# A two-layer graph transformer on one core: the token sums of the seven-product blocks on GpSimd instead of VectorE

## The chip, the cores and the metric

The kernel runs on one core of a Trainium2 chip. The metric is the device time of one execution in microseconds, the median of several runs. TensorE (PE) multiplies, PEld is its weight load, VectorE (DVE) and ScalarE (ACT) work on tiles, GpSimd (POOL) works on tiles too and issues the indirect DMAs (gathers and scatters), SyncE (SP) issues the others.

## The reference

Two layers of a graph transformer over 2708 tokens of width 512, 8 heads, a hidden width of 2048; `adj` is a sparse 0/1 matrix. All numbers are f32.

```python
q, k, v = h @ Wq.T + bq, h @ Wk.T + bk, h @ Wv.T + bv      # 8 heads of 64
scores = where(mask == 0, -1e9, q.k / sqrt(64))
ctx = softmax(scores) @ v
h1 = layer_norm(h + ctx @ Wo.T + bo)
h2 = layer_norm(h1 + relu(h1 @ W1.T + b1) @ W2.T + b2)
```

## The kernel before

**Tiles and blocks.** The tokens are sorted by their number of neighbours and cut into 22 tiles of up to 128. Two tiles make a block, so there are 11 blocks, numbered k = 0 to 10. Layer 0 is done block by block, then layer 1. For each block TensorE does the feed-forward part, and around it the program writes, in the order in which the engines are to do it, the output projection of the next block, the keys and values of the block before for the next layer, and steps of the attention of later blocks.

**Attention.** It runs over lists of neighbours. GpSimd gathers rows of keys and values into the buffers `kv` (line 1113), five buffers of up to two neighbours a token; a gather is issued three steps before it is used. A step of VectorE is: `kv` times `q` (line 1150), its sums per head (`sc`, line 1156, a reduction with one input), and for the step before, values times weights (line 1182) and the accumulation (line 1189). ScalarE makes the weights `p` (line 1169) and scales some of the values (line 1176). When a tile is done its sums follow (lines 1197 to 1212).

**Norms.** Each norm ends on VectorE with line 1273 (the variance, `va`), line 1276 (subtract the mean, times the gain) and line 1281 (times `rd`, plus the shift). In between, GpSimd makes `rd`, the inverse root, from `va` (line 1275). Each block has two norms after the output projection (lines 1455 and 1458 stand ahead of them) and two at its end.

**The seven-product blocks.** In layer 0 the blocks k = 2 to 9 do the second product of the feed-forward part, `relu(..) @ W2.T`, for the first 14 of 16 slices of the hidden width with seven products of half size where eight would be used (a form of Strassen's scheme). The 14 slices are 7 pairs, j = 0 to 6. For slice f TensorE makes `pf` (line 1653, eight instructions, as an f32 product takes two passes), ScalarE the relu `ft` (line 1664). From the two `ft` of a pair, f0 and f1, each with 128 columns for either tile of the block, `sums(j)` makes four sums or differences of 128x128, written to `s[:, 0]`, the upper half of f0 in place, `s[:, 1]` and `s[:, 2]` (lines 1625 to 1628; `s` lies in a tile that the trace calls `forms`). `products(j)` (line 1643) then uses them: `s[:, 1]` in the second product, f0's upper half in the third, `s[:, 0]` in the sixth, `s[:, 2]` in the seventh. Three sums of the weights for each pair are formed once (lines 1592 to 1595) and loaded anew for every block.

**The order around the change.** `sums(j)` is written behind the relu of slice 2j + 2, `products(j)` behind slice 2j + 5. In the loop over f the attention steps, the output projection, and the keys and values are written in between. The last pair's products come after those of slices 14 and 15; then ScalarE and VectorE add up the four PSUM tiles (lines 1695 to 1703), and the two norms follow. So in VectorE's queue the first two sets of sums of a block stand behind the second norm of the block before. TensorE meanwhile does the slices 0 to 5 of the new block, then turns the normed tiles of the block before (line 1293, `tp`), and then needs the first pair's sums.

Of the kernel before, what the change touches and what calls it, by code (L numbers as in the profile page):

```python
# [13 lines left out]
ALU = mybir.AluOpType  # L14
# [4 lines left out]
P = 128  # L19
# [464 lines left out]
def by_edges(ctx: ExitStack, tc: tile.TileContext, x, xT, adj, layers, out, redo):  # L484
# [9 lines left out]
    nc = tc.nc  # L494
# [807 lines left out]
    class Layer:  # L1302
# [310 lines left out]
        def feed_forward_by_seven(self, k, block, hs, hT):  # L1613
# [8 lines left out]
            def sums(j):  # L1622
                f0, f1 = fts[2 * j], fts[2 * j + 1]
                s = self.sums[j % 2]
                nc.vector.tensor_tensor(s[:, 0], f1[:, P:], f0[:, P:], ALU.add)
                nc.vector.tensor_tensor(f0[:, P:], f0[:, :P], f0[:, P:], ALU.subtract)
                nc.vector.tensor_tensor(s[:, 1], s[:, 0], f0[:, :P], ALU.subtract)
                nc.vector.tensor_tensor(s[:, 2], f1[:, :P], s[:, 1], ALU.subtract)

            def products(j):  # L1630
                f0, f1, w, s = fts[2 * j], fts[2 * j + 1], self.w2[j], self.sums[j % 2]
# [17 lines left out]
            for f in range(NFC):  # L1649
                j = f // 2  # L1650
                pf = ps_f.tile([P, DM], F32, tag="f", name="pf")
                for c in range(NC):
                    nc.tensor.matmul(  # L1653
                        pf[:, :W],
                        self.w1[j][:, c, f % 2 * P : f % 2 * P + P],
                        hT[:, c, :],
                        start=(c == 0),
                        stop=(c == NC - 1),
                    )
                if f % 6 < 4:  # L1660
                    ft = dn.tile([P, W], F32, tag="ft", name="ft", bufs=4)
                else:
                    ft = self.more_fts[f % 2]
                nc.scalar.activation(ft, pf[:, :W], AF.Relu, bias=self.b1[:, f : f + 1])  # L1664
                fts.append(ft)
                if f % 2 == 0 and j > 0:
                    sums(j - 1)
                yield None
                if f % 2 and j > 1:
                    products(j - 2)  # L1670
# [411 lines left out]
```

## Time and profile before

| | |
|---|---|
| median of 3 runs (lowest, highest) | 1830.28 us (1830.05, 1832.14) |
| span of the profiled execution, first to last instruction | 1827.1 us |
| around the span, against the median of the runs | 3.2 us |
| granted TensorE clock | 0.999 |
| GpSimd, whole span: busy, instructions | 798.9 us, 745 |
| gathers of `kv` (line 1113): count, busy, mean | 420, 524.0 us, 1248 ns |
| `rd` (line 1275): count, mean | 88, 914 ns |
| the eight seven-product blocks | from 393 to 1005 us of the span |

In the groups of instructions a row gives line, engine, operation, output and inputs, their shapes and the count, then busy time in us and the mean of one in ns, then the idle time ahead of them and who ended it. In the timelines a row gives the start in us, the duration in us, then the same names, and in brackets the idle time before with its releaser. In the waits a row gives who waited for whom, the total, the count and the longest, in us. In the table by stretches each engine has its busy time, in the order PE, PEld, DVE, ACT, POOL, then clock and DMA. Spans on POOL are rough.

### The profile page before, as it was taken

To read this page: it belongs to the slowest core of one execution; us is meant where nothing else is said; L and a number is where in the kernel's file an instruction comes from. 1 tells how busy PE (TensorE), PEld (TensorE's weight loads), DVE (VectorE), ACT (ScalarE), POOL (GpSimd) and SP (SyncE) were. 2 spreads that over 40 slices of the span, in tenths; PEclk is the share of its full clock that TensorE was granted. 3 is DMA by queue.
4 is the path that set the end of the run, shared out by engine and by line. 5 is a ranking of instruction groups with operands and counts; after the bars stand their busy time and mean duration, and the time that the engine had idled before them with its cause. 6 is when DMAs were issued, how large, how long until landed. Compare 5 with 4: busy or idle time off the path is not lost.

```text
span 1827.1 us, 22528 instructions
## 1 busy us (share of the span) xinstructions
PE 1807.5 (99%) x6563; PEld 1162.6 (64%) x6563; DVE 1457.5 (80%) x2447; ACT 949.1 (52%) x3271; POOL 798.9 (44%) x745
## 2 busy tenths in 40 slices
PE   9999999999999999999999999999999999999998
PEld 4444456666777867778677644666666666666666
DVE  5887778988989889898895257887898888889853
ACT  5771435645556545564543213665665565567531
POOL 3334755534455544454430042353464555456302
PEclk9999999999999999999999999999999999999999
DMA  9997987757576676765652876745564664555300
GB/s 340 369 335 256 371 283 245 236 169 241 195 255 228 197 236 196 219 233 181 228 191 70 287 257 248 285 160 180 178 228 150 228 224 169 195 197 194 133 14 21
DMA packets 158061, 393.80 MB, mean 216 GB/s; under 512 B 17514, under 2 KB 60894, under 8 KB 157928
## 3 DMA queue, kind: packets, MB, share of 16 engines
q0 software_dynamic: 70608, 252.12, 40.2%
q1 hardware_dynamic: 77162, 118.55, 18.7%
q10 hardware_dynamic: 10158, 21.61, 3.1%
q8 instruction: 53, 0.87, 0.2%
q14 instruction: 80, 0.66, 0.1%
HBM read 338.78 MB, written 53.44 MB: 215 GB/s over the span
## 4 chain that ended last, share of the span: by engine, by line
PE 89%; DVE 5%; issue 2%; ACT 2%; DMA 1%; POOL 1%; POOLq 0%; SPq 0%; DVEq 0%
PE pf L1523 18%; PE a L1496 17%; PE pf L1653 9%; PE k L620 8%; PE v L620 8%; PE q L620 8%; PE o L620 8%; PE c L1643 4%; PE a L1643 3%; PE tp L1293 2%; DVE sc L1156 1%; DVE kv L1150 1%; DMA forms<-form_d 1%; PE a L1677 1%; PE a L1673 1%
## 5 line engine op out<-in xcount | busy, mean ns | idle before, releaser
L1113 POOL DMA_INDIRECT kv<-kv_d,listed x420 | 524.0, 1248 | 291.2 <-DVE acc L1189 133.9
L1523 PE MATMUL pf<-hT,w 128*128 128x256 f32 (+1 forms) x1792 | 393.2, 367 | 0.1
L1523 PEld LDWEIGHTS pf<-hT,w 128*128 128x128 f32 x1792 | 323.5, 190 | 103.1 <-issue 64.4
L1496 PE MATMUL a<-w,ft 128*128 128x512 f32 x800 | 373.1, 592 | 0.0
L1176 ACT ACTIVATE kv<-kv,p 128x64 f32<-128x64 f32 x1232 | 311.0, 335 | 5.0
L1275 POOL TENSOR_TENSOR rd<-va,mhalf 128x1 f32<-128x1 f32 (+1 forms) x88 | 80.5, 914 | 520.6 <-DVE va L1273 520.5
L1150 DVE TENSOR_TENSOR kv<-kv,q 128x1024 f32<-128x1024 f32 (+1 forms) x222 | 256.9, 1157 | 13.3 <-DMA q<-q_d,ident_i 10.9
L1156 DVE TENSOR_REDUCE sc<-kv 128x16 f32<-128x1024 f32 (+1 forms) x222 | 257.9, 1162 | 7.6
L1189 DVE TENSOR_TENSOR acc<-acc,kv 128x1024 f32<-128x1024 f32 (+2 forms) x178 | 205.4, 1154 | 37.6 <-ACT kv L1176 23.0
L1653 PE MATMUL pf<-hT,w 128*128 128x256 f32 x1024 | 233.1, 379 | 1.6 <-ACT ft L1664 1.6
L1496 PEld LDWEIGHTS a<-w,ft 128*128 128x128 f32 x800 | 150.1, 190 | 113.2 <-issue 101.3
L1653 PEld LDWEIGHTS pf<-hT,w 128*128 128x128 f32 x1024 | 193.9, 190 | 35.4 <-issue 7.9
L1534 ACT ACTIVATE ft<-pf,b 128x256 f32<-128x256 f32 (+1 forms) x208 | 95.0, 459 | 197.6 <-PE pf L1523 195.2
L1169 ACT ACTIVATE p<-sc,listed 128x8 f32<-128x8 f32 x420 | 104.0, 296 | 147.2 <-DVE sc L1156 135.7
L620 PE MATMUL o<-wo,cT 128*128 128x512 f32 x336 | 151.0, 593 | 1.0 <-ACT cT L1298 1.0
L1664 ACT ACTIVATE ft<-pf,b 128x256 f32<-128x256 f32 x96 | 44.9, 468 | 160.5 <-PE pf L1653 160.5
L1182 DVE TENSOR_TENSOR kv<-kv,p 128x512 f32<-128x512 f32 (+1 forms) x178 | 123.4, 693 | 4.5 <-ACT p L1169 4.3
L620 PEld LDWEIGHTS o<-wo,cT 128*128 128x128 f32 x336 | 63.4, 190 | 74.7 <-issue 65.5
L745 DVE MAX8 tops<-code 128x8 f32<-128x247 f32 (+2 forms) x242 | 78.6, 400 | 28.3 <-ACT code L740 28.3
L1281 DVE SCALAR_TENSOR_TENSOR h<-h,rd,ln_b 128x512 f32<-128x512 f32 (+1 forms) x88 | 65.9, 749 | 39.5 <-POOL rd L1275 39.5
L1220 ACT ACTIVATE cx<-acc,su 128x64 f32<-128x64 f32 (+1 forms) x352 | 88.2, 333 | 12.9 <-DVE su L1212 7.4
L1455 DVE TENSOR_TENSOR h<-o,xb 128x512 f32<-128x512 f32 (+1 forms) x44 | 30.3, 688 | 80.0 <-PE o L620 65.0
(232 smaller groups left out, 2323.5 us busy)
## 6 DMA issues: line engine op xcount, KB each, us to landing
aj<-in_adj SPq DMA_DIRECT2D x42, 677.0 KB, 6.3
forms<-form_d SPq DMA_DIRECT2D x168, 128.0 KB, 4.2
kv_d<-kvs ACTq DMA_DIRECT2D x21, 512.0 KB, 5.5
xg<-in_xT SPq DMA_DIRECT2D x19, 512.0 KB, 7.4
w<-in_W SPq DMA_DIRECT2D x16, 512.0 KB, 6.2
kv<-kv_d,listed POOLq DMA_INDIRECT x420, 6.3
zT_d<-zT SPq DMA_DIRECT2D x22, 256.0 KB, 5.1
xb_d<-h SPq DMA_DIRECT2D x21, 256.0 KB, 5.7
```

Of the source, the lines that this page charges most:

```text
L620: nc.tensor.matmul(o[:r], xs(c), wm[:, c, :], start=(c == 0), stop=(c == NC - 1))
L1113: return nc.gpsimd.indirect_dma_start(out=to, out_offset=None, in_=table[:, :], in_offset=bass.IndirectOffsetOnAxis(ap=s, axis=0), bounds_ ...
L1150: nc.vector.tensor_tensor(kv[:r, :c, :DM], kv[:r, :c, :DM], self.q[:r].unsqueeze(1).to_broadcast([r, c, DM]), ALU.mult,)
L1156: nc.vector.tensor_reduce(self.sc[:r, s0 : s0 + c, :], kv[:r, :c, :DM].rearrange("p s (h d) -> p s h d", d=DK), AX.X, ALU.add,)
L1169: nc.scalar.activation(p[:r, s, :], self.sc[:r, s, :], AF.Exp, bias=minus[:r, g, s : s + 1])
L1176: nc.scalar.activation(to[:, i, hd], kv[:r, i, DM + h * DK : DM + (h + 1) * DK], AF.Copy, scale=p[:r, s0 + i, h : h + 1],)
L1182: nc.vector.tensor_tensor(to[:, 0, :].rearrange("p (h d) -> p h d", d=DK), kv[:r, 0, DM:].rearrange("p (h d) -> p h d", d=DK), p[:r, s0, : ...
L1189: nc.vector.tensor_tensor(self.acc[:r, :c, :], self.acc[:r, :c, :], kv[:r, :c, DM:], ALU.add)
L1496: nc.tensor.matmul(a[:r, cols], fts[f][:, c0 : c0 + r], self.w2[f // 2][:, f % 2, cols], start=(f == 0), stop=(f == NFC - 1),)
L1523: nc.tensor.matmul(pf[:, :w], self.w1[f // 2][:, c, f % 2 * P : f % 2 * P + P], hT[:, c, :w], start=(c == 0), stop=(c == NC - 1),)
L1643: nc.tensor.matmul(to, left, right, start=start, stop=stop)
L1653: nc.tensor.matmul(pf[:, :W], self.w1[j][:, c, f % 2 * P : f % 2 * P + P], hT[:, c, :], start=(c == 0), stop=(c == NC - 1),)
```

## The change

The four additions and subtractions of `sums(j)` are issued by GpSimd instead of VectorE; operands, shapes and the place in the program stay.

```diff
             def sums(j):
                 f0, f1 = fts[2 * j], fts[2 * j + 1]
                 s = self.sums[j % 2]
-                nc.vector.tensor_tensor(s[:, 0], f1[:, P:], f0[:, P:], ALU.add)
-                nc.vector.tensor_tensor(f0[:, P:], f0[:, :P], f0[:, P:], ALU.subtract)
-                nc.vector.tensor_tensor(s[:, 1], s[:, 0], f0[:, :P], ALU.subtract)
-                nc.vector.tensor_tensor(s[:, 2], f1[:, :P], s[:, 1], ALU.subtract)
+                nc.gpsimd.tensor_tensor(s[:, 0], f1[:, P:], f0[:, P:], ALU.add)
+                nc.gpsimd.tensor_tensor(f0[:, P:], f0[:, :P], f0[:, P:], ALU.subtract)
+                nc.gpsimd.tensor_tensor(s[:, 1], s[:, 0], f0[:, :P], ALU.subtract)
+                nc.gpsimd.tensor_tensor(s[:, 2], f1[:, :P], s[:, 1], ALU.subtract)
```

The instructions of TensorE and ScalarE keep their order. First VectorE at the start of block k = 5, before, from the second closing norm of block 4 on:

```order
L1276 SCALAR_TENSOR_TENSOR h<-h,mv,ln_g 128x512
L1281 SCALAR_TENSOR_TENSOR h<-h,rd,ln_b 128x512
L1625 TENSOR_TENSOR forms<-ft 128x128
L1626 TENSOR_TENSOR ft<-ft 128x128
L1627 TENSOR_TENSOR forms<-forms,ft 128x128
L1628 TENSOR_TENSOR forms<-ft,forms 128x128
L1625 TENSOR_TENSOR forms<-ft 128x128
L1626 TENSOR_TENSOR ft<-ft 128x128
L1627 TENSOR_TENSOR forms<-forms,ft 128x128
L1628 TENSOR_TENSOR forms<-ft,forms 128x128
L1150 TENSOR_TENSOR kv<-kv,q 128x2x512
L1156 TENSOR_REDUCE sc<-kv 128x16
```

VectorE at the same place now:

```order
L1276 SCALAR_TENSOR_TENSOR h<-h,mv,ln_g 128x512
L1281 SCALAR_TENSOR_TENSOR h<-h,rd,ln_b 128x512
L1150 TENSOR_TENSOR kv<-kv,q 128x2x512
L1156 TENSOR_REDUCE sc<-kv 128x16
L1182 TENSOR_TENSOR kv<-kv,p 128x512
L1189 TENSOR_TENSOR acc<-acc,kv 128x1024
```

The two sets of sums (j = 0 and 1) are gone; the attention step follows the norm directly. GpSimd at the same place, before:

```order
L1275 TENSOR_TENSOR rd<-va,mhalf 128x1 x2
L1113 DMA kv<-kv_d_111,listed 128x1024 x2
L1113 DMA xb<-in_x,ident_i 128x512 x2
L1113 DMA kv<-kv_d_111,listed 128x1024 x4
L1113 DMA q<-q_d_113,ident_i 128x512
```

and now:

```order
L1275 TENSOR_TENSOR rd<-va,mhalf 128x1 x2
L1625 TENSOR_TENSOR forms<-ft 128x128
L1626 TENSOR_TENSOR ft<-ft 128x128
L1627 TENSOR_TENSOR forms<-forms,ft 128x128
L1628 TENSOR_TENSOR forms<-ft,forms 128x128
L1625 TENSOR_TENSOR forms<-ft 128x128
L1626 TENSOR_TENSOR ft<-ft 128x128
L1627 TENSOR_TENSOR forms<-forms,ft 128x128
L1628 TENSOR_TENSOR forms<-ft,forms 128x128
L1113 DMA kv<-kv_d_111,listed 128x1024 x2
L1113 DMA xb<-in_x,ident_i 128x512 x2
```

The sums stand behind both `rd` of the closing norms and ahead of the gathers. Later in the same block GpSimd had, behind the scatters of the next layer's keys and values, six gathers and the two `rd` of the norms after the output projection:

```order
L1113 DMA kv<-kv_d_111,listed 128x1024 x2
L1076 DMA kv_d_112<-kvs,ident_i 2708x1024 x2
L1113 DMA kv<-kv_d_111,listed 128x1024 x6
L1275 TENSOR_TENSOR rd<-va,mhalf 128x1 x2
L1113 DMA kv<-kv_d_111,listed 128x1024 x4
```

and has now, from the fourth of these gathers on:

```order
L1113 DMA kv<-kv_d_111,listed 128x1024 x4
L1625 TENSOR_TENSOR forms<-ft 128x128
L1626 TENSOR_TENSOR ft<-ft 128x128
L1627 TENSOR_TENSOR forms<-forms,ft 128x128
L1628 TENSOR_TENSOR forms<-ft,forms 128x128
L1113 DMA kv<-kv_d_111,listed 128x1024 x2
L1275 TENSOR_TENSOR rd<-va,mhalf 128x1
L1625 TENSOR_TENSOR forms<-forms 128x128
L1626 TENSOR_TENSOR forms<-forms 128x128
L1627 TENSOR_TENSOR forms<-forms 128x128
L1628 TENSOR_TENSOR forms<-forms 128x128
L1275 TENSOR_TENSOR rd<-va,mhalf 128x1
```

The sums of j = 4 stand ahead of the last two gathers and the first `rd`, those of j = 5 between the two `rd`.

## The prediction

> **What bounds the kernel now.** I read the page's busy times first, then the stretch in which the edited lines run (393 to 1005 us, the eight seven-product blocks), then what TensorE waits for inside it.
>
> ```profile
> PE 1807.5 (99%) x6563; PEld 1162.6 (64%) x6563; DVE 1457.5 (80%) x2447; ACT 949.1 (52%) x3271; POOL 798.9 (44%) x745
> 393.00:1005.00 612.00, 605.68 (x2492) 453.72 (x2491) 525.72 (x878) 324.84 (x1211) 273.04 (x225) 1.00 0.62 203
> PE o L615 <- ACT cT L1298: 2.4, 1, 2.4
> PE tp L1293 <- DVE h L1281: 1.8, 2, 1.0
> PE pf L1653 <- ACT ft L1664: 1.6, 2, 0.8
> ```
>
> The reader is to see that TensorE is the bound, in the whole span and in this stretch (605.68 of 612 us). The last three rows are its waits of any size there: 5.8 us, of which VectorE causes 1.8 (two waits for a normalized tile, line 1281). No row has TensorE waiting for lines 1625 to 1628. So taking work off VectorE can give back about 2 us, while any operand that comes later than TensorE wants it costs its full lateness.
>
> How late may the sums come? I looked for the tightest of the seven pairs of a block and found the first: its sums are made at the block's start, right behind the two norms that end the block before. Here is block k = 5, as VectorE, GpSimd and the weight loads have it.
>
> ```profile
> 631.39 0.74 DVE L1276 SCALAR_TENSOR_TENSOR h<-h,mv,ln_g 128x512 f32<-128x512 f32 x1
> 632.58 0.75 DVE L1281 SCALAR_TENSOR_TENSOR h<-h,rd,ln_b 128x512 f32<-128x512 f32 x1 [0.45 <-POOL rd L1275]
> 633.25 0.28 DVE L1625 TENSOR_TENSOR forms<-ft 128x128 f32<-128x128 f32 x1
> ...
> 633.78 0.28 DVE L1627 TENSOR_TENSOR forms<-forms,ft 128x128 f32<-128x128 f32 x1
> ...
> 635.36 1.22 DVE L1150 TENSOR_TENSOR kv<-kv,q 128x1024 f32<-128x1024 f32 x1
> 636.61 1.22 DVE L1156 TENSOR_REDUCE sc<-kv 128x16 f32<-128x1024 f32 x1
> 631.62 0.93 POOL L1275 TENSOR_TENSOR rd<-va,mhalf 128x1 f32<-128x1 f32 x1 [1.25 <-DVE va L1273]
> 634.26 0.41 PEld L1643 LDWEIGHTS c<-forms 128*128 128x128 f32 x2
> ```
>
> Call E the end of the last norm's line 1281: 632.58 + 0.75 = 633.33. The third add (line 1627) makes s[:,1], the weights of the second product; it ends at 633.78 + 0.28 = 634.06, E + 0.73, and TensorE loads it at 634.26. The slack is 0.20 us. The first and the last of the eight blocks:
>
> ```profile
> 405.95 0.28 DVE L1627 TENSOR_TENSOR forms<-forms,ft 128x128 f32<-128x128 f32 x1
> 406.29 0.39 PEld L1643 LDWEIGHTS c<-forms 128*128 128x128 f32 x2
> 937.75 0.28 DVE L1627 TENSOR_TENSOR forms<-forms,ft 128x128 f32<-128x128 f32 x1
> 939.09 0.41 PEld L1643 LDWEIGHTS c<-forms 128*128 128x128 f32 x2
> ```
>
> That is 0.06 and 1.06; read off the same two rows, blocks k = 2 to 9 have 0.06, 0.05, 1.37, 0.20, 0.21, 0.69, 0.09 and 1.06 us, 3.73 together. The later pairs of a block are not as tight: see the last one of block 5, below.
>
> **The change, part by part.** Removed from VectorE: 56 times four adds.
>
> ```profile
> L1626 DVE TENSOR_TENSOR ft<-ft 128x128 f32<-128x128 f32 x40 | 11.9, 297 | 1.4
> ```
>
> This is the slowest of the eight groups of these lines; 224 adds at 0.297 us are at most 66 us of VectorE time. What of that is on the path? In block 5 the stretch from the last attended norm to the block's closing sums (line 1696) shows it:
>
> ```profile
> 680.95 0.69 DVE L1455 TENSOR_TENSOR h<-o,xb 128x512 f32<-128x512 f32 x1 [2.35 <-PE o L620]
> 685.34 0.29 DVE L1625 TENSOR_TENSOR forms<-ft 128x128 f32<-128x128 f32 x1
> 686.47 1.22 DVE L1150 TENSOR_TENSOR kv<-kv,q 128x1024 f32<-128x1024 f32 x1
> 690.37 1.22 DVE L1189 TENSOR_TENSOR acc<-acc,kv 128x1024 f32<-128x1024 f32 x1 [0.82 <-ACT kv L1176]
> 695.20 1.25 DVE L1189 TENSOR_TENSOR acc<-acc,kv 128x1024 f32<-128x1024 f32 x1 [0.58 <-ACT kv L1176]
> 687.43 0.47 ACT L1664 ACTIVATE ft<-pf,b 128x256 f32<-128x256 f32 x1 [4.28 <-PE pf L1653]
> 696.51 0.41 PEld L1643 LDWEIGHTS c<-forms 128*128 128x128 f32 x2
> ```
>
> VectorE waits for TensorE at 680.95 and twice for ScalarE, which itself had waited 4.28 us for TensorE. The 1.13 us of one set of sums (685.34 to 686.47) would only lengthen the wait at 690.37. (These are the sums of the last pair, done before 686.6 and loaded at 696.51: 10 us of room.) So I put the gain from the relief at zero, except after block 2, where no such wait lies between the last sums and the block's end: there 1.13 less about 0.5 for collisions (below), 0.6 us.
>
> Added to GpSimd: 224 adds. None of this shape in f32 is in the trace; the nearest are a 128x128 add of integers and a 128x512 one of f32.
>
> ```profile
> L734 POOL TENSOR_TENSOR aj<-aj,diag 128x128 int32<-128x128 int32 x20 | 8.7, 433 | 29.6 <-DMA aj<-in_adj 29.6
> L958 POOL TENSOR_TENSOR kvs<-kvs,bk 128x512 f32<-128x512 f32 x20 | 25.4, 1272 | 52.4 <-ACT kvs L956 43.3 <-issue 4.7 <-DMA aj<-in_adj 4.3
> ```
>
> I take 0.43 us, since the shape is the same; a quarter of the second row would be 0.32. By the skill an add would be longer: the Trainium skill, GPSIMD Engine Reference, section Engine selection, puts two-input elementwise work about 2x slower on GpSimd than on VectorE, which makes an estimate of 0.59 us an add and, by the steps below, 10.6 us in place of 6.7. The trace has 1.5x (0.43 against 0.297), and I go by it.
>
> Moved: the adds now stand in GpSimd's queue directly behind the two rd instructions (line 1275) of the block's start, and VectorE goes from line 1281 straight to line 1150. Do the engines get in each other's way? These rows say so:
>
> ```profile
> 447.83 0.58 POOL L1275 TENSOR_TENSOR rd<-va,mhalf 128x1 f32<-128x1 f32 x1
> 142.42 1.25 POOL L958 TENSOR_TENSOR kvs<-kvs,bk 128x512 f32<-128x512 f32 x1
> 142.60 1.64 DVE L771 TENSOR_TENSOR hot<-count,by 128x528 f32<-128x528 f32 x1
> ```
>
> An rd that runs alone takes 0.58 us. The one at 631.62 started while line 1276 (two inputs in SBUF) ran, took 0.93, and ended at 632.55, 0.42 after line 1276's end at 632.13: of its 0.58, 0.16 had passed before it was held. The other way, line 771 started 0.18 after a GpSimd add and took 1.64 for 528 columns, ending 0.57 after that add. So a GpSimd add and a two-input VectorE instruction do not overlap; the second waits for the first. Who goes when both wait? A scatter of GpSimd, which takes 1.02 alone, between two such instructions:
>
> ```profile
> 436.28 1.02 POOL L1076 DMA_INDIRECT kv_d<-kvs,ident_i  x1 [0.30 <-issue]
> 437.61 1.60 POOL L1076 DMA_INDIRECT kv_d<-kvs,ident_i  x1 [0.31 <-issue]
> 437.11 1.23 DVE L1189 TENSOR_TENSOR acc<-acc,kv 128x1024 f32<-128x1024 f32 x1
> 438.25 1.22 DVE L1150 TENSOR_TENSOR kv<-kv,q 128x1024 f32<-128x1024 f32 x1
> ```
>
> The second scatter ended 0.87 after line 1189 and was not held by line 1150 as well, which was ready by then: the one that has waited longer goes first, and so they take turns. If nothing were held, the three adds would end at 632.55 + 3 x 0.43 = 633.84, before 634.06, and nothing would be late. The Trainium skill, SBUF — State Buffer, section Who interferes with whom, has the holding as a rule: a VectorE instruction with two SBUF inputs and a GpSimd instruction that reads SBUF share an interface, and whichever is issued first keeps it to its end. By that rule the time would come out as forecast below; the trace agrees in both directions (0.93 against 0.58, and 1.64).
>
> The steps at the block's start, from E: add 1 is held by line 1281 until E and needs 0.43 - 0.16 = 0.27 more: E + 0.27. Line 1150, ready since E - 0.08 as the first add was before, runs its remaining 1.14: E + 1.41. Add 2, held behind it, 0.27: E + 1.68. Add 3 runs beside line 1156, which has one input, in 0.43: E + 2.11. Before it was E + 0.73, so s[:,1] comes 1.38 us later. Less each block's slack, TensorE waits 1.32, 1.33, 0.01, 1.18, 1.17, 0.69, 1.29 and 0.32, which is 7.3 us; less 0.6 for the relief in front of block 3, **6.7 us**. The fourth add (s[:,2], the seventh product) has five products of 0.43 more and is hidden by them.
>
> Bounds: if no add is ever held, nothing is late and the 1.8 us of waits for line 1281 could go: -2 us. If add 3 too is held by a full 1.22 us instruction and then needs 0.27, it ends at E + 3.17, 2.44 later than before: 8 x 2.44 - 3.73 - 0.6 = +15 us. I take 6.7, which has a row for each hold.
>
> What else is queued behind the adds on GpSimd:
>
> ```profile
> 671.29 1.40 POOL L1113 DMA_INDIRECT kv<-kv_d,listed  x1 [0.30 <-issue]
> 675.76 0.93 POOL L1275 TENSOR_TENSOR rd<-va,mhalf 128x1 f32<-128x1 f32 x1 [0.42 <-DVE va L1273]
> 683.65 0.92 POOL L1275 TENSOR_TENSOR rd<-va,mhalf 128x1 f32<-128x1 f32 x1 [6.96 <-DVE va L1273]
> 688.95 1.04 PE L1293 MATMUL tp<-ident,h 128*128 128x128 f32 x8
> ```
>
> The fifth set of sums stands between the gather that ends at 672.69 and the rd at 675.76, with two gathers between. Four adds of 0.8 us would move that rd by about 3 us, to 679; its reader on VectorE is followed by line 1455, which waits for TensorE until 680.95 anyway. The sixth set stands between the two rd's and has until 683.65. TensorE reads the normed tiles at 688.95. So this is hidden, with about 3 us to spare. Gathers are issued three steps ahead of their reader; 3 us of delay stays inside that.
>
> **Against the runs.** The profiled span is 1827.1 us, 3.2 under the median of the runs (1830.28), which holds what lies around it. I add to the median: 1830.28 + 6.7 = 1837.0 us. A measurement of this kernel can tell 0.2%, 3.7 us, from no change.
>
> **Rivals.**
> - *Back to back, no change.* GpSimd, once it has the interface, keeps it: adds 2 and 3 follow at 0.43 each, E + 1.13, only 0.40 later than before. Stalls: 0.34 + 0.20 + 0.19 + 0.31, block 3 covered by its relief: 1.0 us, 1831.3. For it: GpSimd's adds have no other engine to wait for. Against: line 1150 is ready before add 2 is. Chance 0.20.
> - *VectorE's relief counts, faster.* If ScalarE's waits shrink with VectorE's, the norms come 1 us earlier in each block, the late sums are covered and most of the waits of 2.4, 1.8 and 1.6 us go: some -5, 1825.3. Against: the rows at 680.95, 687.43 and 690.37. Chance 0.07.
> - *GpSimd's queue becomes the bound, far slower.* If four adds take over 5 us instead of some 3, the rd's are late. At 6 us: sums to 678.69, two gathers of 1.3, rd to 682.3, sums to 688.3, rd to 689.2, line 1281 to 690.0, 0.6 behind the second half of the reads from 688.95; seven blocks, 4 us. At that pace three adds at the block's start take 4.5, ending 3.0 later than before: 8 x 3.0 - 3.73 = 20. Together +24, 1854. Chance 0.06.
> - That the change doesn't do what it says is excluded: the instruction order shows the 224 adds on GpSimd.
>
> **How the numbers follow.** The forecast has 0.67, nearly all of it over 3.7 us (0.05 within). Faster 0.07; same 0.20 + 0.05 = 0.25; slower 0.62 + 0.06 = 0.68. The range takes the likely bound above (+15 us) and the no-change rival, down to 1829.5, leaving out most of the two outer rivals: 1829.5 to 1845.5.
>
> **What would show it.** Right: in the changed profile, a wait of about 1.2 us of TensorE or its weight loads for line 1627 at the start of most blocks, none at the later pairs; line 1150 at 0.27 behind E or its duration near 1.5; the second add lasting over 1 us; rd in the attended norms 2 to 4 us later with nothing behind it. Wrong: line 1627 ending by E + 1.2; or waits for lines 1625 to 1628 at pairs other than the first; or the closing norms of a block sooner after the last product than now.

## The result and the profile after

| | before | changed |
|---|---|---|
| median of 20 runs each (lowest, highest), one chip | 1829.72 us (1828.66, 1835.99) | 1835.51 us (1832.47, 1840.51) |
| ratio, 95% interval | | 1.0029 (1.0021 to 1.0036) |
| median of two later groups of runs | 1829.25; 1830.04 us | 1834.84; 1835.07 us |
| their ratios | | 1.0030 (1.0018 to 1.0042); 1.0026 (1.0017 to 1.0035) |

The change costs 5.3 us (0.0029 x 1829.72), between 3.8 and 6.6. The forecast was +6.7 us. The two later groups are two of the experiments below, with the changed kernel untouched. One execution of the kernel with two more adds ahead of the fourth pair (below) took 11025 us and is left out of its ratio; the median of its other five is 1837.48 us.

The busy times of the page, then the stretch of the eight seven-product blocks, which is 621 us long in the profiled execution and was 612:

```profile
PE 1809.9 (99%) x6563; PEld 1161.7 (63%) x6563; DVE 1418.9 (77%) x2223; ACT 948.3 (52%) x3271; POOL 934.6 (51%) x969
```

```profile
393.00:1014.00 621.00, 609.98 (x2496) 453.69 (x2495) 488.89 (x656) 326.21 (x1219) 410.68 (x449) 1.00 0.61 201
```

VectorE gave up 36.8 us of busy time in the stretch (525.72 to 488.89), GpSimd took on 137.6 (273.04 to 410.68), and TensorE still has 99% of the span. The profiled spans differ by 8.8 us (1827.1 and 1835.9), more than the medians: this execution took 1837.65 us, 2.1 above its kernel's median, and some 2 us of the difference lie ahead of 393 us, where nothing was changed. The later profiles of the same kernel have spans of 1831.9 and 1831.0 us.

TensorE's waits between 393 and 1015 us, and below them the same for its weight loads over the whole span:

```profile
PE c L1643 <- POOL forms L1627: 3.3, 6, 0.6
PE o L615 <- ACT cT L1298: 2.3, 1, 2.3
PE c L1643 <- DMA forms<-form_d: 2.0, 2, 1.3
PE pf L1653 <- ACT ft L1664: 1.7, 2, 0.8
PE tp L1293 <- DVE h L1281: 1.7, 2, 1.1
```

```profile
PEld c L1643 <- POOL forms L1627: 5.9, 7, 1.0
```

The first row is the new one: six waits for line 1627, the third add, now on GpSimd. The rows for lines 615, 1653 and 1293 stand as they were (2.4, 1.6, 1.8 before). Now block 5 again, VectorE, GpSimd, weight loads and TensorE from the last norm on:

```profile
637.67 0.94 DVE L1281 SCALAR_TENSOR_TENSOR h<-h,rd,ln_b 128x512 f32<-128x512 f32 x1 [0.45 <-POOL rd L1275]
638.54 1.48 DVE L1150 TENSOR_TENSOR kv<-kv,q 128x1024 f32<-128x1024 f32 x1
640.05 1.22 DVE L1156 TENSOR_REDUCE sc<-kv 128x16 f32<-128x1024 f32 x1
...
637.61 0.45 POOL L1625 TENSOR_TENSOR forms<-ft 128x128 f32<-128x128 f32 x1
638.14 0.79 POOL L1626 TENSOR_TENSOR ft<-ft 128x128 f32<-128x128 f32 x1
638.89 1.43 POOL L1627 TENSOR_TENSOR forms<-forms,ft 128x128 f32<-128x128 f32 x1
640.40 0.46 POOL L1628 TENSOR_TENSOR forms<-ft,forms 128x128 f32<-128x128 f32 x1
...
640.38 0.30 PEld L1643 LDWEIGHTS c<-forms 128*128 128x128 f32 x2 [0.98 <-POOL forms L1627]
...
639.20 0.60 PE L1643 MATMUL a<-forms,ft 128*128 128x256 f32 x2
640.38 0.70 PE L1643 MATMUL c<-forms 128*128 128x256 f32 x2 [0.58 <-POOL forms L1627]
640.92 0.59 PE L1643 MATMUL c<-forms,ft 128*128 128x256 f32 x2
```

An add that nothing holds takes 0.45 us. Add 1 started 0.06 ahead of line 1281 and wasn't held; line 1281 was, and took 0.94 instead of 0.75. Add 2 then ended at 638.93, 0.32 behind the end of line 1281 at 638.61: held by it. Line 1150 was held by add 2 (1.48 instead of 1.22). Add 3 stood beside line 1150, which ended at 640.02, and ended itself 0.30 after that. The two engines took turns, one instruction each, and all eight blocks have the same four end times within 0.02 us: -0.55, 0.32, 1.71 and 2.24 after the end of line 1281.

The same three products of TensorE before the change:

```profile
634.04 0.60 PE L1643 MATMUL a<-forms,ft 128*128 128x256 f32 x2
634.48 0.59 PE L1643 MATMUL c<-forms 128*128 128x256 f32 x2
634.91 0.59 PE L1643 MATMUL c<-forms,ft 128*128 128x256 f32 x2
```

The distance from the first product to the second was 0.44 us and is now 1.18: the second starts 0.74 late, although its weight load waited 0.98. From the first to the third it was 0.87 and is now 1.72: the third starts 0.85 late. The missing 0.1 us lies inside the second product, whose two passes start 0.32 us apart instead of 0.22.

### The profile page after: what moved, and what is told of

It reads as the page before. It is cut to its first block, busy times and chain, and to the rows that moved or that the text cites. A ratio compares the mean times of both kernels' runs of the same rounds, so it can differ in the third digit from the quotient of the medians.

```text
span 1835.9 us, 22631 instructions
## 1 busy us (share of the span) xinstructions
PE 1809.9 (99%) x6563; PEld 1161.7 (63%) x6563; DVE 1418.9 (77%) x2223; ACT 948.3 (52%) x3271; POOL 934.6 (51%) x969
## 4 chain that ended last, share of the span: by engine, by line
PE 80%; DVE 7%; issue 4%; ACT 4%; POOL 3%; DMA 2%; SPq 0%; POOLq 0%; DVEq 0%; ACTq 0%
PE pf L1523 17%; PE a L1496 17%; PE k L620 8%; PE v L620 8%; PE pf L1653 7%; PE o L620 7%; PE q L620 6%; PE c L1643 4%; PE a L1643 3%; ACT kv L1176 2%; PE tp L1293 2%; DVE kv L1150 1%; DVE sc L1156 1%; DMA forms<-form_d 1%; POOL rd L1275 1%
## 5 line engine op out<-in xcount | busy, mean ns | idle before, releaser
L1113 POOL DMA_INDIRECT kv<-kv_d,listed x420 | 504.3, 1201 | 200.1 <-issue 105.8
L1150 DVE TENSOR_TENSOR kv<-kv,q 128x1024 f32<-128x1024 f32 (+1 forms) x222 | 262.6, 1183 | 15.5 <-DMA q<-q_d,ident_i 12.2
L1455 DVE TENSOR_TENSOR h<-o,xb 128x512 f32<-128x512 f32 (+1 forms) x44 | 30.3, 689 | 81.2 <-PE o L620 67.9
```

The source lines that it names most:

```text
L1113: return nc.gpsimd.indirect_dma_start(out=to, out_offset=None, in_=table[:, :], in_offset=bass.IndirectOffsetOnAxis(ap=s, axis=0), bounds_ ...
L1150: nc.vector.tensor_tensor(kv[:r, :c, :DM], kv[:r, :c, :DM], self.q[:r].unsqueeze(1).to_broadcast([r, c, DM]), ALU.mult,)
```

## The experiments

My theory, A: the price lies only where a block starts, since TensorE asks for the first pair's sums there at once, and it comes from the two engines' turns; the other pairs' sums cost nothing, and VectorE's relief is worth nothing. Rival B: the price is spread over all sets, through GpSimd's longer queue or through VectorE instructions that last longer beside its adds. Rival C: the relief of VectorE is worth something, and the price at the blocks' starts hides it. Each ratio is against the kernel before on the same chip: its median is 1829.22 us beside the first four kernels below (late pairs, first pairs, one-input instructions, two more adds ahead of the first pair), 1830.04 beside the two more adds run again, the ten more and the changed kernel of that group, and 1829.25 beside the rest. In the edited kernels the numbers of the lines behind the edit are one to three higher.

### Late pairs on GpSimd, the first two on VectorE

```diff
-                nc.gpsimd.tensor_tensor(s[:, 0], f1[:, P:], f0[:, P:], ALU.add)
+                by = nc.vector if j < 2 else nc.gpsimd
+                by.tensor_tensor(s[:, 0], f1[:, P:], f0[:, P:], ALU.add)
...
```

> GpSimd makes the sums of pairs 2 to 6 of each block (40 of the 56 sets), VectorE those of pairs 0 and 1 as before the change. Theory A (only the set that stands at a block's start has a price, because TensorE waits for it and for no other; relief of VectorE is worth next to nothing): the time falls back to that of the kernel before, 1829.7 us within 1.5, and PEld shows no wait for line 1627 on GpSimd at a block's start (5.9 us in 7 places in the changed kernel). Theory B (the price lies on all sets alike, through GpSimd's longer queue or through VectorE's instructions that last longer beside it): 40/56 of the +5.3 us stay, about 1833.5. Theory C (relief of VectorE counts and was only covered by the price at the blocks' starts): faster than before, below 1827.

Measured: 1827.86 us, ratio 0.9994 (0.9985 to 1.0003). All of the price is gone, with 40 of the 56 sets still on GpSimd. TensorE's waits in the stretch, and the table's row for 393 to 1005 us:

```profile
PE o L615 <- ACT cT L1298: 2.2, 1, 2.2
PE pf L1654 <- ACT ft L1665: 1.6, 2, 0.8
PE tp L1293 <- DVE h L1281: 1.3, 2, 0.9
```

```profile
393.00:1005.00 612.00, 606.75 (x2502) 454.84 (x2501) 496.22 (x720) 324.88 (x1212) 378.49 (x385) 1.00 0.61 204
```

The three rows are those of before. VectorE is 29.5 us less busy (525.72 to 496.22), GpSimd 105 more, and TensorE does about as much in the 612 us as before (606.75, 605.68). Against B. The median lies 1.4 us under that of before, but the interval holds 1.

### The complement: the first two pairs on GpSimd

```diff
+                by = nc.gpsimd if j < 2 else nc.vector
+                by.tensor_tensor(s[:, 0], f1[:, P:], f0[:, P:], ALU.add)
...
```

> The complement: GpSimd makes the sums of pairs 0 and 1 of each block (16 of 56 sets), VectorE all others. Theory A: nearly the whole price is there, +4 to +5.5 us, 1834 to 1835.3, and PEld waits some 6 us for line 1627 in 7 or 8 places, as in the changed kernel. Theory B: 16/56 of +5.3 us, +1.5, about 1831.2. Theory C: slower than the changed kernel, since the price stays and the relief goes: above 1836.

Measured: 1836.35 us, ratio 1.0037 (1.0023 to 1.0051): 16 of the 56 sets carry the whole price. The weight loads' wait:

```profile
PEld c L1644 <- POOL forms L1628: 5.8, 7, 1.0
```

It is the changed kernel's (5.9, 7 times, line number shifted by one). The median lies above what A named (1835.3), but the interval, +4.2 to +9.3 us, holds it. Theory C asked for a time above 1836 as well, so this run alone doesn't part A from C; the run without sums does.

### One-input instructions where line 1150 stood

```diff
                 s = self.sums[j % 2]
+                if j == 0:
+                    for _ in range(3):
+                        spread(self.e2)
                 nc.gpsimd.tensor_tensor(s[:, 0], f1[:, P:], f0[:, P:], ALU.add)
```

> The changed kernel with three more one-input instructions on VectorE (the kernel's own statistics instruction over a constant that it reads anyway, into a scratch tile, about 0.69 us each) ahead of sums(0) in each block, so that VectorE's two-input line 1150 doesn't stand beside GpSimd's adds at a block's start. Theory A with the hold (add 3 took 1.43 us because a two-input VectorE instruction ran beside it): add 3 lasts 0.45 to 0.6 us, the adds end about 0.8 us after the end of line 1281 and not 2.24, PEld's waits for line 1627 fall from 5.9 us to under 1.5, and the time comes back to within 2 us of the kernel before, 1830 to 1832. Rival (GpSimd's add is slow by itself, or starts late after the semaphore): the wait stays near 1 us in a block and the time at 1835 to 1837.

Measured: 1829.17 us, ratio 1.0002 (0.9993 to 1.0011). All 56 sets are on GpSimd, VectorE even does three instructions more in each block, and the price is gone. Block 5:

```profile
632.96 0.44 POOL L1628 TENSOR_TENSOR forms<-ft 128x128 f32<-128x128 f32 x1
633.48 0.79 POOL L1629 TENSOR_TENSOR ft<-ft 128x128 f32<-128x128 f32 x1
634.23 0.46 POOL L1630 TENSOR_TENSOR forms<-forms,ft 128x128 f32<-128x128 f32 x1
...
633.01 0.94 DVE L1281 SCALAR_TENSOR_TENSOR h<-h,rd,ln_b 128x512 f32<-128x512 f32 x1 [0.45 <-POOL rd L1275]
633.88 1.87 DVE L1286 BATCH_NORM_STATS2 st<-ln_b 128x6 f32<-128x512 f32 x3
635.66 1.20 DVE L1150 TENSOR_TENSOR kv<-kv,q 128x1024 f32<-128x1024 f32 x1
...
634.74 0.41 PEld L1646 LDWEIGHTS c<-forms 128*128 128x128 f32 x2
```

Adds 1 and 2 last as long as in the changed kernel. Add 3 (here line 1630), beside the statistics with one input, lasts 0.46 instead of 1.43 and ends 0.74 after line 1281, where it ended 0.73 after it before the change; the weights are loaded without a wait. So the price was the hold of add 3 by line 1150, all of it as far as the interval tells (-1.3 to +2.0 us). GpSimd's longer adds, add 2's hold and line 1281's 0.19 us cost nothing that can be measured.

### Two more adds ahead of the first pair, and ahead of the fourth

```diff
+                if j == 0:
+                    for _ in range(2):
+                        nc.gpsimd.tensor_tensor(s[:, 2], f1[:, P:], f0[:, P:], ALU.add)
                 nc.gpsimd.tensor_tensor(s[:, 0], f1[:, P:], f0[:, P:], ALU.add)
```

> The changed kernel with two more adds of 128x128 on GpSimd ahead of add 1 of pair 0 of each block, which repeat add 1 into a part of the tile that add 4 overwrites. Theory A (the chain of four adds at a block's start stands on the path, and nothing absorbs a delay of it): two unheld adds of 0.45 us come on top, the second sum is ready some 0.9 us later in each of eight blocks, +6 to +8 us over the changed kernel, about 1842; where one of them is held by line 1150 as well, up to 1849. Theory B (the price is spread over GpSimd's queue, and the block start is no special place): 16 adds more on 224, +0.4 us, about 1836.

Measured: 1842.44 us, ratio 1.0069 (1.0056 to 1.0083), 7 us over the changed kernel. The weight loads' waits, then block 5:

```profile
PEld c L1646 <- POOL forms L1630: 13.3, 8, 2.0
```

```profile
638.02 1.44 POOL L1628 TENSOR_TENSOR forms<-ft 128x128 f32<-128x128 f32 x1
639.53 0.46 POOL L1629 TENSOR_TENSOR ft<-ft 128x128 f32<-128x128 f32 x1
639.95 0.45 POOL L1630 TENSOR_TENSOR forms<-forms,ft 128x128 f32<-128x128 f32 x1
```

The third of six adds meets line 1150 and lasts 1.44; the fourth and fifth run beside line 1156 in 0.46 and 0.45. s[:,1] is ready 2.66 after the end of line 1281, 0.95 later than in the changed kernel; eight times that is 7.6, and the loads' wait rose by 7.4 (5.9 to 13.3).

The same two adds with `j == 3` in place of `j == 0`:

> The changed kernel with two more adds on GpSimd as in the run that put them ahead of pair 0 (that one cost some 7 us over the changed kernel), but ahead of pair 3, whose sums were ready 3.5 us or more before TensorE asked for them. Theory A (a delay counts only where no slack is left): the time of the changed kernel, within 1.5 us, about 1835. Theory B (GpSimd's queue, or what its adds do to VectorE, has the price wherever they stand): the same +7 us as at pair 0, about 1842.

Measured: 1837.53 us, ratio 1.0046 (1.0033 to 1.0059), and beside it the changed kernel untouched:

> The changed kernel once more, beside the others of this group: +4 to +6.5 us over the kernel before, some 1835. It also tells whether the waits of TensorE for the forms that come from DRAM by DMA (PEld 2.8 us in the first profile after, 2.4 with the first pairs alone on GpSimd, 1.3 in the other two experiments on the changed kernel) belong to the change: if they follow from it, PEld's wait for forms lies again above 2 us; if they vary from run to run, anywhere between 0.4 and 3.

Measured: 1834.84 us, ratio 1.0030 (1.0018 to 1.0042). The wait of its weight loads for forms that come by DMA is 0.9 us here; it was 2.8 in the first profile of the same kernel, and the third lists none. So it varies from run to run and isn't the change's. (A further 0.9 us in this profile is put down to line 1625, but the load that waits there, for pair 2 of block 7, reads none of the sums that ran then.)

The 2.7 us between the two kernels were more than A's 1.5 and less than B's 7; no row of the trace named a wait for pair 3. So it was run again on another chip, with the changed kernel beside it and a stronger dose:

> The two more adds ahead of pair 3 once more. Theory A: within 1.5 us of the changed kernel beside it, the 2.7 us of the first time being the runs' scatter; if they were a price, +2 to +3.5 us again.

> The changed kernel as the measure for the run with ten more adds in a block, on the same chip: 1834 to 1836, ratio to the kernel before 1.003.

Measured: 1835.89 us, ratio 1.0025 (1.0014 to 1.0035), against 1835.07 us, 1.0026 (1.0017 to 1.0035). Here the difference is 0.8 us: two adds cost 7 us ahead of the first pair, and by the medians 0.8 and 2.7 us ahead of the fourth, which these runs hardly tell from nothing. The traces hint at a small price. The loads' wait for the first pair's sums is the same in both profiles with the two adds, and 5.9 in all three of the changed kernel:

```profile
PEld c L1646 <- POOL forms L1630: 6.6, 7, 1.0
```

The 0.7 us more all lie at block 9, where the load waits 0.94 instead of 0.20.

### Ten more adds in a block

The edit of the last section with `j > 1`: 80 more adds in all.

> The two more adds on GpSimd ahead of pair 3 came out 2.7 us above the changed kernel beside them (medians), inside the two intervals but more than theory A's 1.5; their trace shows no wait for the sums of pair 3. Here two more adds stand ahead of each of the pairs 2 to 6, 80 in all, five times the dose, each pair's slack being 3.5 us or more. If GpSimd's load has a price away from the block's start, five times 2.7: +13 us over the changed kernel, about 1848. Theory A: the changed kernel's time within 2 us, about 1835 to 1837, with PEld's waits for GpSimd's sums still near 6 us.

Measured: 1845.04 us, ratio 1.0074 (1.006 to 1.0088), 10 us over the changed kernel beside it. Here theory A fails in the strict form that I gave it. The waits in the stretch, of this kernel and of the changed kernel beside it:

```profile
PE tp L1293 <- DVE h L1281: 5.8, 5, 1.7
PE c L1646 <- POOL forms L1630: 3.9, 7, 0.6
PE c L1646 <- DMA forms<-form_d: 2.5, 4, 1.0
```

```profile
PE c L1643 <- POOL forms L1627: 3.3, 6, 0.6
...
PE tp L1293 <- DVE h L1281: 1.7, 2, 1.1
```

The sums' own wait hardly moved (3.9 against 3.3), and no late pair's sums are waited for. What grew is the wait for normed tiles (1.7 to 5.8; four of the five waits stand at a block's start) and that for forms that come by DMA (no such row to 2.5; as the first profile of the changed kernel had 2.0, this one may be scatter). So GpSimd's load does have a price away from the first pair. It isn't one price for every add: the 224 of the change cost nothing that can be told once the hold at the block's start is gone (the one-input run), and these 80 cost 10 us. But those came off VectorE, and these came on top. Where the price sets in isn't shown: at 10 us for 80, the 16 adds of the last section would cost 2.

VectorE's waits between 393 and 1015 us tell in part where the late norms come from; this kernel first, then the changed kernel beside it:

```profile
DVE h L1281 <- POOL rd L1275: 47.0, 25, 8.5
DVE h L1281 <- POOL rd L1275: 30.7, 25, 4.5
```

The 16.3 us more all lie in the seven waits for the first `rd` of a block's attended norms, each 1.7 to 4.0 us longer, while line 1150 lasts 1.26 us on average instead of 1.23. So GpSimd's queue ahead of `rd` looks like the larger part, rather than the holds in VectorE's attention steps; it wasn't tried by itself.

### The sums left out

Pairs 2 to 6 of seven blocks get no sums (35 of 56 sets; their products use old ones), the rest on VectorE.

```diff
+                if j > 1 and k > FORMED + 1:
+                    return
+                nc.vector.tensor_tensor(s[:, 0], f1[:, P:], f0[:, P:], ALU.add)
...
```

> The sums back on VectorE as before the change, and those of pairs 2 to 6 in seven of the eight blocks left out (35 of the 56 sets; the products of these pairs use old sums, so the output isn't the reference's). This takes VectorE's load off, about 35 x 1.19 = 42 us, without putting it anywhere else, and leaves the set at a block's start where it was. Theory A (relief of VectorE is worth next to nothing, since TensorE waits for VectorE in few places): 1827 to 1829.7, 0 to -2 against before. Theory C (relief counts, and GpSimd's own price hid it): -5 us or more, below 1825.

Measured: 1828.36 us, ratio 0.9998 (0.999 to 1.0007).

```profile
393.00:1005.00 612.00, 606.47 (x2504) 455.19 (x2503) 493.94 (x740) 325.44 (x1212) 270.68 (x225) 1.00 0.61 203
```

VectorE lost 31.8 us of work in the stretch (525.72 to 493.94) that no other engine took up, and the time stayed, within 1.8 us. Theory C asked for 5 us or more: it falls.

### Only the first pair on VectorE

```diff
+                by = nc.vector if j < 1 else nc.gpsimd
...
```

> VectorE makes the sums of pair 0 of each block alone, GpSimd those of the other six pairs (48 of 56 sets). Theory A (the one set at a block's start carries the whole price): the time of the kernel before, within 1.5 us, no PEld wait for GpSimd's sums, though six sevenths of the change stay. If pair 1 had a share in the price as well, which the run with pairs 0 and 1 on VectorE couldn't tell: above 1831, with PEld waits for its sums. Theory B (spread over all sets): 48/56 of the price, 1834.

Measured: 1831.14 us, ratio 1.0013 (1.0004 to 1.0021): +2.4 us, between 0.7 and 3.8. A had asked for no price, and B for 1834. Block 5:

```profile
633.12 0.45 POOL L1626 TENSOR_TENSOR forms<-ft 128x128 f32<-128x128 f32 x1
633.65 0.79 POOL L1627 TENSOR_TENSOR ft<-ft 128x128 f32<-128x128 f32 x1
634.40 0.50 POOL L1628 TENSOR_TENSOR forms<-forms,ft 128x128 f32<-128x128 f32 x1
...
633.18 0.94 DVE L1281 SCALAR_TENSOR_TENSOR h<-h,rd,ln_b 128x512 f32<-128x512 f32 x1 [0.45 <-POOL rd L1275]
634.05 0.54 DVE L1626 TENSOR_TENSOR forms<-ft 128x128 f32<-128x128 f32 x1
634.62 0.43 DVE L1627 TENSOR_TENSOR ft<-ft 128x128 f32<-128x128 f32 x1
634.97 0.28 DVE L1628 TENSOR_TENSOR forms<-forms,ft 128x128 f32<-128x128 f32 x1
...
635.30 0.30 PEld L1644 LDWEIGHTS c<-forms 128*128 128x128 f32 x2 [0.44 <-DVE forms L1628]
```

The adds on GpSimd here are those of pair 1. TensorE doesn't wait for them, but they run at the same moment as VectorE's adds of pair 0 and hold those: 0.54 and 0.43 instead of 0.28 each, so that s[:,1] ends 1.13 after line 1281 and not 0.73, and the weight load waits 0.44. The loads' wait for these sums is 2.6 us in 6 places. So the place that costs is not a set of sums but a moment: two-input work on GpSimd in the half microsecond in which VectorE has the first pair's sums to make costs as well.

## Why the prediction was right

**TensorE as the bound, and the relief at zero.** Right. Without 31.8 us of VectorE's work the time moved by less than 0.2%, and the waits that VectorE causes (1.8 us before, 1.7 after) stayed. In the changed kernel VectorE waits longer instead: 30.3 us for ScalarE at line 1189 (17.9 before) and 31.1 for `rd` (13.8 before).

**Only the first pair of a block is tight.** Right for the waits: the changed kernel's trace has none for another pair's sums. As a rule for the price it was too narrow, as pair 1's adds in the way of pair 0's showed, and the 80 adds at the late pairs.

**The add's price, 0.43 us.** Right: 0.45 unheld. An estimate of 0.59 us and +10.6 us stood beside it, from the Trainium skill, GPSIMD Engine Reference, section Engine selection (about 2x slower than VectorE). The traces have 0.45 against 0.28, 1.6x, so the measurement decides against that page's figure at this size.

**The holds and the turns.** The mechanism was right, the order wrong. The step that failed was "add 1 is held by line 1281 until E". Add 1 came 0.06 us first in block 5 and held line 1281, whose end moved by 0.19. Everything behind it moved up one place: add 2 was held by line 1281 where I had line 1150, and add 3 by line 1150 where I had it free. s[:,1] came 1.71 behind the new E, 1.90 behind the old one, where I had 2.11: a shift of 1.17 us and not 1.38. That the wrong order cost only 0.21 us is partly luck: in both orders just one instruction as long as line 1150 stands between E and s[:,1], where the upper bound of +15 us had two. The rule of the Trainium skill, SBUF — State Buffer, section Who interferes with whom, that the one issued first keeps the interface to its end, agrees with 0.94, 0.79, 1.48 and 1.43 here. That the one that has waited longer goes next agrees with the turns too. The scatter from which I had it doesn't show it: line 1150 took its usual 1.22 us beside the rest of the scatter, so the two ran side by side there.

**The stalls, 7.3 us.** Mis-sized, in two steps. With the shift of 1.17 the same slacks give 5.8 us, and the weight loads do wait 5.9, though block by block the two are up to 0.14 apart. But I had taken a late weight load for an equally late product. In block 5 the load waited 0.98, and the products behind it are 0.85 late. Over the blocks, the third product's distance from the first is 0.87 to 0.89 us too long in five of them, 0.47 in one and 0.06 in another, 5.0 and 4.9 us together in the two later profiles of the changed kernel (the second product's own start, 4.3). If I take all products between 393 and 1015 us and add up by how much each starts later than the usual distance for its shape, before has 11.2 us and the changed kernel 16.6 and 16.3 in the later profiles: +5.4 and +5.1, which is the measured +5.3. Nearly all of that are the late sums.

**What makes up the rest, some 0.3 us.** Away from those starts the products of line 1643 are 1.3 us late in all before the change, and 1.5 and 1.6 in the later profiles. They were 0.7 and 1.1 us in two runs where the block's start wasn't late (the late pairs on GpSimd, and the one-input instructions), so a difference of 0.3 is within what these runs vary by. Some of the lateness is a wait for forms that come by DMA; in the first profile after the change that wait was 2.0 us, which explains part of that execution's length. The change didn't alter the number of these loads.

**The relief ahead of block 3, -0.6 us.** Mis-sized: the turned tile there comes 0.37 us sooner (1.15 to 0.78 us late in the later profile), but that ahead of block 2 comes 0.18 later (1.03 to 1.21), as line 1281 is held by add 1 for 0.19.

**What else waits on GpSimd.** Right: the first `rd` of the attended norms in block 5 stands here in the changed kernel:

```profile
684.07 0.58 POOL L1275 TENSOR_TENSOR rd<-va,mhalf 128x1 f32<-128x1 f32 x1
```

Against E it comes 3.0 us later than before (684.07 - 638.61 = 45.46, against 675.76 - 633.33 = 42.43), as forecast. VectorE does wait for it: its waits for `rd` in the stretch are 31.1 us instead of 13.8, the longest 4.5 instead of 1.5. But TensorE's waits for normed tiles stay (1.8 us before, 1.7 after). The rival in which GpSimd's queue becomes the bound didn't come, but it is not far off: with 80 adds more TensorE waits 4 us longer for normed tiles, and the time is 10 us up.

**The other rivals.** Back to back was wrong for the reason given: line 1150 does get its turn. That VectorE's relief makes the kernel faster was tried by itself and found to be nothing. No version here beats the kernel before by more than can be told apart: late pairs alone on GpSimd has 0.9994 (0.9985 to 1.0003).

## What to carry to other kernels

Before work is moved to a less busy engine, look for the one instance of it that the bounding engine asks for at once, and for what the engine it leaves does at that moment: 40 of these 56 sets moved for nothing, and the other 16 carried the whole price. Two-input work on VectorE and on GpSimd took turns here, so the instruction that comes up beside the moved one decides: add 3 lasted 1.43 us beside a two-input instruction and 0.46 beside a one-input one, and that made the same move free. Room on the other engine isn't endless either: 80 adds more cost 10 us. A late weight load isn't an equally late product (0.98 against 0.85 here), so stalls are best summed from the starts of the products behind it.

## What the runs showed of the hardware

- The hold goes both ways within one chain, and the engines alternate: an unheld 128x128 f32 add of 0.45 us on GpSimd lasted 0.79 behind line 1281's rest and 1.43 behind line 1150, while line 1281 lasted 0.94 instead of 0.75 and line 1150 1.48 instead of 1.22. Beside one-input instructions (line 1156, line 1286) the adds took 0.45 to 0.46.
- Small VectorE adds suffer as much: 0.54 instead of 0.28 us for 128x128 beside an add of GpSimd.
- Over the stretch the third and second add lasted 2.2 and 1.6 times their unheld 0.45 us on average (40 of the 56 sets; the other 16 have other tile names):

```profile
L1627 POOL TENSOR_TENSOR forms<-forms,ft 128x128 f32<-128x128 f32 x40 | 39.0, 975 | 0.0
L1626 POOL TENSOR_TENSOR ft<-ft 128x128 f32<-128x128 f32 x40 | 29.6, 741 | 3.2
```

- A product whose weight load is late starts its second pass late too: its two passes start 0.32 us apart instead of 0.22 (block 5, and five other blocks in each of the three profiles of the changed kernel).
- Who comes first is a matter of 0.06 us, and yet it came out the same way in all eight blocks and in all three profiles of the changed kernel, within 0.02 us: -0.55, 0.32, 1.71 and 2.24 after line 1281.
